# Inverse row transforms at a kernel's end: loads through another queue, five buffers, four ahead, and two groups kept for last

## The chip, the cores and the metric

The kernel runs on one core of a Trainium2 chip. The metric is the device time of one execution in microseconds (us); lower is better. The core has TensorE (PE, with its weight loads listed as PEld), VectorE (DVE), ScalarE (ACT), GpSimd (POOL), and SyncE (SP), which here only issues transfers. All transfers run on the core's 16 DMA engines. An engine works through its own instructions in order; between engines, semaphores are waited for.

## The reference

The input is an image of 48 x 48 tokens with 768 channels in float32. It passes two layers. The first is a transformer block with relative positions and full attention, and an MLP:

```python
xn = layernorm(x, ln1_g, ln1_b)
qkv = xn.reshape(B, H * W, C) @ qkv_w + qkv_b
...
x = shortcut + out
xn2 = layernorm(x, ln2_g, ln2_b)
h = jax.nn.gelu(xn2 @ mlp_w1 + mlp_b1, approximate=False)
return x + (h @ mlp_w2 + mlp_b2)
```

The second, which ends the kernel, goes to the frequencies of rows and columns, applies two small complex matrix layers there in 8 blocks of 96 channels, comes back and adds its input:

```python
xf = jnp.fft.rfft2(x.astype(jnp.float32), axes=(1, 2), norm='ortho')
...
o1r = jax.nn.relu(mm(xr, w1[0]) - mm(xi, w1[1]) + b1[0])
o1i = jax.nn.relu(mm(xi, w1[0]) + mm(xr, w1[1]) + b1[1])
o2r = _softshrink(mm(o1r, w2[0]) - mm(o1i, w2[1]) + b2[0], SPARSITY)
o2i = _softshrink(mm(o1i, w2[0]) + mm(o1r, w2[1]) + b2[1], SPARSITY)
...
y = jnp.fft.irfft2(z.reshape(B, H, Wh, C), s=(H, W), axes=(1, 2), norm='ortho')
return y.astype(x.dtype) + bias
```

## The kernel before

All arithmetic is in float32. A Fourier transform is a matmul with a constant matrix. The tokens stay on the chip throughout in `x1`, 18 tiles of 128 tokens by 768 channels.

**MLP and forward row transforms.** The MLP runs in three passes of 768 tokens. At the end of each, `rows_forward` (L1050) makes the row transform of that pass's tokens: for each half of the channels (384, index k) and each of two groups of 384 tokens, four results `zp` (L1057) from six matmuls. Each is copied to a tile `zt` of 100 x 384 (L1061), of which there are eight, and stored to the DRAM tensor z1 of its half (L1066, z<-zt). In the first two passes ScalarE makes the copies, in the third VectorE and ScalarE in turn.

**Frequencies.** 14 units follow, seven for each half of the channels, each with up to four column frequencies. A unit passes four stages: `columns` (forward column transform, fp at L1178), `first` (first layer, lp at L1197 and L1198), `second` (second layer, mp at L1221) and `back` (inverse column transform, yp at L1240). They are interleaved: round r does `columns` of unit r, `first` of unit r-1, `second` of unit r-2 and `back` of unit r-3, in four steps i of one quarter each. There are 17 rounds. `load` fetches zi from z1 (L926); `back` stores its results y to the DRAM tensor z2 of the half (L1246, z<-y). The last unit of each half has one frequency only, so the last `back` is one yp, in round 16.

**Inverse row transforms.** `rows_back` (L1250) does one group of 384 tokens of one half: a load of 600 KB from z2 to zo (100 partitions x 4 x 384, L1253), then three pieces. A piece is two matmuls into rps (L1261), VectorE's addition of x1 into yt (L1264, four buffers) and a store of 192 KB to the output (L1265). A half has six groups. Because a group needs every frequency of its half, the first half's groups can start once its z2 is complete, during the second half's units, and the second half's groups only after the last yp.

zo has three buffers, and loads and stores all go through SP's queue. `rows_back` is a Python generator that stops after the load and after each piece. `pieces` runs the generators of a half one after another: a group's load is called right before its first piece. The loop takes one such step at each i from round 12 on (L1284), so the first half's groups 0 to 3 are worked off among the second half's units; groups 4 and 5 and the second half's six come after the last yp.

**What sets the order.** TensorE's instructions stand in the order of the Python program (`manual_schedule` for PE). For the other engines and queues a scheduler places the instructions at build time, and gives a tile a buffer of its pool when an earlier tile has been released; the buffers are thus passed on in the order in which the program asks for them. The semaphores of transfers are eight, used in turn, and a transfer also waits for the one that used its semaphore last.

Of the kernel before, what the change touches and what calls it, by code (L numbers as in the profile page):

```python
# [9 lines left out]
F32 = mybir.dt.float32  # L10
# [8 lines left out]
P = 128  # L19
HW = 48  # L20
T = HW * HW
# [8 lines left out]
G = 384  # L30
NB = 8
BS = C // NB
CH = C // 2
KW = HW // 2 + 1
# [10 lines left out]
def block_then_afno(  # L45
# [25 lines left out]
    nc = tc.nc  # L71

    def balanced_copy(i, dst, src):
        if i % 2:
            nc.scalar.copy(dst, src)
        else:
            nc.vector.tensor_copy(dst, src)
# [111 lines left out]
    with ExitStack() as flag_scope:  # L189
# [11 lines left out]
        with ExitStack() as att:  # L201
# [331 lines left out]
            with tc.manual_schedule(engines={mybir.EngineType.PE, mybir.EngineType.SP}):  # L533
# [70 lines left out]
                for n, (pr, c, u) in enumerate(runs):  # L604
# [19 lines left out]
                    if pr < NC - 1:  # L624
                        if (c, u) in ((3, 1), (4, 0), (4, 1)):
                            i = 2 * (2 * (c - 3) + u - 1)
# [55 lines left out]
        with tc.tile_pool(name="ps_flag", bufs=1, space=PSUM) as psum, tc.tile_pool(  # L682
            name="ps_early", bufs=2, space=PSUM
# [29 lines left out]
        with tc.If(safe < 1):  # L713
            with ExitStack() as att:
                xnT = main.rearrange("p (c t) -> p c t", c=NC)
                with tc.tile_pool(name="g_ln1", bufs=3) as ln1, tc.tile_pool(
                    name="g_ps_ln1", bufs=2, space=PSUM
# [197 lines left out]
    turn = ctx.enter_context(tc.tile_pool(name="turn", bufs=6))  # L915
    first_loads = []

    def load_frequencies(half, k0):

        rows = z1[half].rearrange("(r k) c -> r k c", k=KW)  # L920
        tiles = []
        for k in range(k0, min(k0 + 4, KW), 2):
            n = min(2, KW - k)
            zi = turn.tile([P, C], F32, name="zi", tag="turn")
            zi = zi[: 2 * HW].rearrange("p (k c) -> p k c", c=CH)
            nc.sync.dma_start(out=zi[:, :n], in_=rows[:, k : k + n, :])  # L926
            tiles.append(zi)
        return tiles

    with ExitStack() as mlp:  # L930
# [119 lines left out]
        def rows_forward(p):  # L1050

            for k in range(2):
                for g in (2 * p, 2 * p + 1):
                    for a, parts in enumerate(((0,), (1, 2), (3, 4), (5,))):
                        zp = psum.tile([2 * 2 * KW, CH], F32, name="zp", tag=f"o{a}")
                        for b in parts:
                            nc.tensor.matmul(  # L1057
                                zp, rows_dft[:, b, :], x1[:, 3 * g + b // 2, ts(k, CH)],
                                start=(b == parts[0]), stop=(b == parts[-1]),
                            )  # L1060
                        zt = turn.tile([2 * 2 * KW, CH], F32, name="zt", bufs=8)  # L1061
                        if p < 2:
                            nc.scalar.copy(zt, zp)
                        else:
                            balanced_copy(a, zt, zp)
                        nc.sync.dma_start(out=z1[k][ts(4 * g + a, 4 * KW), :], in_=zt)  # L1066
                if (p, k) == (2, 0):
                    first_loads.extend(load_frequencies(0, k0) for k0 in (0, 4))
# [21 lines left out]
        with tc.manual_schedule(engines={mybir.EngineType.PE}):  # L1090
            for p in range(T // TB):
                for n in range(n_f):
                    work = hidden(p, n)
                    for i in range(3):
                        next(work)
                        if n:
                            added(p, n - 1, i)
                    if p < 2 and 4 <= n < 10:
                        normalised(p + 1, n - 4)
                for i in range(3):  # L1100
                    if p < 2:
                        turned(i)
                    added(p, n_f - 1, i)
                if p < 2:
                    sums_of_tokens(xt, xs)
                rows_forward(p)

    with ExitStack() as sp:
        psum = sp.enter_context(tc.tile_pool(name="ps_spec", bufs=2, space=PSUM))
        cst = sp.enter_context(tc.tile_pool(name="spec_const", bufs=1))  # L1110
        zin = sp.enter_context(tc.tile_pool(name="spec_in", bufs=2))
# [137 lines left out]

        def rows_back(half, g):  # L1250

            zo = zin.tile([4 * KW, 4, CH], F32, name="zo", bufs=3)
            nc.sync.dma_start(  # L1253
                out=zo, in_=z2[half][ts(g, 16 * KW), :].rearrange("(a p) c -> p a c", a=4)
            )
            yield
            for i in range(3):
                yt = mid.tile([P, CH], F32, name="yt", bufs=4)
                rp = psum.tile([P, CH], F32, name="rps", tag="f")
                for e in range(2):  # L1260
                    nc.tensor.matmul(  # L1261
                        rp, irows[:, 2 * i + e, :], zo[:, i + e, :], start=(e == 0), stop=(e == 1)
                    )
                nc.vector.tensor_tensor(yt, rp, x1[:, 3 * g + i, ts(half, CH)], ALU.add)  # L1264
                nc.sync.dma_start(out=out[ts(3 * g + i, P), ts(half, CH)], in_=yt)  # L1265
                yield

        units = [Unit(half, k0) for half in range(2) for k0 in range(0, KW, 4)]
        ends = [[rows_back(half, g) for g in range(T // G)] for half in range(2)]

        def pieces(gens):
            for gen in gens:
                yield from gen

        with tc.manual_schedule(engines={mybir.EngineType.PE}):
            first_half = pieces(ends[0])
            for r in range(len(units) + 3):
                if r < len(units):
                    units[r].load()
                for i in range(4):  # L1280
                    for stage, lag in (("back", 3), ("second", 2), ("first", 1), ("columns", 0)):
                        if 0 <= r - lag < len(units):
                            getattr(units[r - lag], stage)(i)
                    if r > len(units) // 2 + 4:  # L1284
                        next(first_half, None)
            for _ in first_half:
                pass
            for _ in pieces(ends[1]):
                pass


# [126 lines left out]
```

## Time and profile before

| | us |
|---|---|
| median of 3 runs | 2955.97 |
| lowest and highest of these | 2951.86, 2956.34 |
| profiled execution, its own time | 2962.34 |
| span from its first to its last instruction | 2960.5 |
| TensorE busy | 2902.6 |
| VectorE busy | 1768.2 |
| ScalarE busy | 881.1 |
| GpSimd busy | 610.2 |
| mean granted clock of TensorE | 0.995 of full speed |

The profile is one execution. Busy times of different engines lie beside one another; they don't add up to the span. The counts of PE are of passes: a matmul in float32 is two, so a piece of the inverse row transforms appears as four. The page divides the span into 40 slices of 74 us, with a digit for each in tenths busy. A finer view gives, for stretches of one's choice, the busy time of each engine, the granted clock and the DMA share. The chain of waits goes back from the last instruction, at each step to what released it. In a list of waits, the name behind the arrow is what ended the wait.

### The profile page before, as it was taken

To read this page: it belongs to the slowest core of one execution; us is meant where nothing else is said; L and a number is where in the kernel's file an instruction comes from. 1 tells how busy PE (TensorE), PEld (TensorE's weight loads), DVE (VectorE), ACT (ScalarE), POOL (GpSimd) and SP (SyncE) were. 2 spreads that over 40 slices of the span, in tenths; PEclk is the share of its full clock that TensorE was granted. 3 is DMA by queue.
4 is the path that set the end of the run, shared out by engine and by line. 5 is a ranking of instruction groups with operands and counts; after the bars stand their busy time and mean duration, and the time that the engine had idled before them with its cause. 6 is when DMAs were issued, how large, how long until landed. Compare 5 with 4: busy or idle time off the path is not lost. (4 is left out here: it accounts for less than half of the span.)

```text
span 2960.5 us, 40962 instructions
## 1 busy us (share of the span) xinstructions
PE 2902.6 (98%) x15771; PEld 1762.2 (60%) x15771; DVE 1768.2 (60%) x2548; ACT 881.1 (30%) x1372; POOL 610.2 (21%) x564
## 2 busy tenths in 40 slices
PE   6999999999999999999999999999999999999998
PEld 4555655555556555555555555555555555557995
DVE  4342327777777777777633666675666566665443
ACT  1011125555556555565500210122011211111210
POOL 2302110000000000000043223342332323322441
PEclk9999999999999999999999999999999999999999
DMA  3423275173461725535252111112111211213225
GB/s 119 150 83 123 88 163 123 26 135 64 75 132 33 139 42 97 113 50 89 59 177 75 42 54 54 64 62 68 54 64 60 75 49 64 64 57 93 83 83 174
DMA packets 202817, 253.03 MB, mean 85 GB/s; under 512 B 21618, under 2 KB 180978, under 8 KB 201078
## 3 DMA queue, kind: packets, MB, share of 16 engines
q1 hardware_dynamic: 202614, 250.32, 33.2%
q8 instruction: 127, 2.08, 0.3%
q14 instruction: 76, 0.62, 0.1%
HBM read 136.40 MB, written 50.14 MB: 63 GB/s over the span
## 5 line engine op out<-in xcount | busy, mean ns | idle before, releaser
L619 DVE TENSOR_TENSOR acc<-acc,main 128x768 f32<-128x768 f32 x576 | 551.9, 958 | 202.0 <-ACT main L562 145.4
L562 ACT ACTIVATE main<-sp 128x768 f32<-128x768 f32 x648 | 522.1, 811 | 155.8 <-PE sp L558 148.6
L558 PE MATMUL sp<-terms,select 64*128 64x384 f32 x1296 | 413.1, 630 | 0.0
L1032 DVE TENSOR_TENSOR main<-o,main 128x384 f32<-128x384 f32 x540 | 299.4, 556 | 41.0 <-PE o L1030 2.1
L970 PE MATMUL h<-shared,w 128*128 128x384 f32 x864 | 296.6, 486 | 0.8 <-issue 0.8
L552 PE MATMUL sp<-shared 64*128 64x384 f32 x1296 | 267.9, 490 | 2.2 <-DVE o L452 2.2
L552 PE MATMUL sp<-qT,kT 64*128 64x384 f32 x1296 | 266.5, 487 | 0.0
L597 POOL TENSOR_TENSOR inverse<-inverse,rden 128x384 f32<-128x384 f32 x36 | 46.3, 1287 | 1031.6 <-DVE rden L594 961.6
L441 PE MATMUL m<-main 128*128 128x384 f32 x756 | 248.4, 490 | 6.2 <-DVE main L172 2.9
L970 PEld LDWEIGHTS h<-shared,w 128*128 128x128 f32 x864 | 164.4, 190 | 116.1 <-issue 2.2
L970 PE MATMUL h<-shared,w1s 128*128 128x384 f32 x648 | 226.6, 486 | 0.0
L567 PE MATMUL op<-main,shared 128*64 128x384 f32 x1296 | 221.3, 488 | 0.0
L567 PE MATMUL op<-main,v 128*64 128x384 f32 x1296 | 219.9, 488 | 0.0
L441 PEld LDWEIGHTS m<-main 128*128 128x128 f32 x756 | 143.4, 191 | 108.7 <-issue 10.1
L976 ACT ACTIVATE hT<-c,vec 128x384 f32<-128x384 f32 x108 | 66.4, 615 | 466.1 <-DVE c L982 466.0
L982 DVE TENSOR_TENSOR c<-h,u 128x384 f32<-128x384 f32 x108 | 60.2, 557 | 212.4 <-PE h L970 212.4
L1030 PE MATMUL o<-w,hT 128*128 128x384 f32 x432 | 175.2, 487 | 3.7 <-DVE mv L118 2.0
L1030 PE MATMUL o<-w2s,hs 128*128 128x384 f32 x432 | 174.9, 487 | 1.4 <-DVE hs L155 1.3
L558 PEld LDWEIGHTS sp<-terms,select 64*128 64x128 f32 x1296 | 125.6, 187 | 84.1 <-issue 0.5
L970 PEld LDWEIGHTS h<-shared,w1s 128*128 128x128 f32 x648 | 123.1, 190 | 85.9
L154 POOL TENSOR_TENSOR w1s<-w 128x384 f32<-128x384 f32 x36 | 36.2, 1006 | 612.5 <-PE o L1030 420.8
L552 PEld LDWEIGHTS sp<-shared 64*128 64x128 f32 x1296 | 117.7, 187 | 60.3 <-issue 23.1
(150 smaller groups left out, 3892.3 us busy)
## 6 DMA issues: line engine op xcount, KB each, us to landing
w<-in_mlp_w_dram SPq DMA_DIRECT2D x72, 768.0 KB
terms<-col_parts SPq DMA_DIRECT2D x432, 72.0 KB
terms<-row_hi SPq DMA_DIRECT2D x216, 72.0 KB
terms<-row_lo SPq DMA_DIRECT2D x216, 72.0 KB
main<-in_qkv_w_dram SPq DMA_DIRECT2D x36, 384.0 KB
z<-zt SPq DMA_DIRECT2D x48, 150.0 KB
zo<-z SPq DMA_DIRECT2D x12, 600.0 KB
x<-in_x_dram SPq DMA_DIRECT2D x18, 384.0 KB
```

Of the source, the lines that this page charges most:

```text
L441: nc.tensor.matmul(bank, a[:, c, :], b[:, c, :], start=(first and c == 0), stop=(c == 2), skip_group_check=not first,)
L552: nc.tensor.matmul(sp[:, j, :G], kT[at, ts(kt, P)], qT[at, ts(c, G)], start=True, stop=False,)
L558: nc.tensor.matmul(sp[:, j, :G], select[at, a % 2], ready[pr, c][at, a // 2, b], start=False, stop=True,)
L562: nc.scalar.activation(p, sp[:, :, :G], AF.Exp, scale=HD**-0.5)
L567: nc.tensor.matmul(op[ts(j, 64)], v[:, kt0 + i, ts(j, 64)], ps[i][:, j, :], start=(kt0 + i == 0), stop=(kt0 + i == NT - 1),)
L597: nc.gpsimd.tensor_tensor(inverse, inverse, rden, ALU.add)
L619: nc.vector.tensor_tensor(acc, made[0] if kt == 1 else acc, p, ALU.add)
L970: nc.tensor.matmul(bank[i], a[:, c, :], b[:, c, :], start=(start and c == 0), stop=(c == 2), skip_group_check=not start,)
L976: nc.scalar.activation(h[:, i, ts(k, G)], src, AF.Gelu, bias=col(V_B1 + 2 * n + i))
L982: nc.vector.tensor_tensor(t, src, other, ALU.add)
L1030: nc.tensor.matmul(bank[k], a, b, start=start, stop=True, skip_group_check=not start)
L1032: nc.vector.tensor_tensor(dst, bank[k], dst, ALU.add)
```

## The change

The loads of the second half's groups are issued by ScalarE in place of SP. Groups whose number over both halves (0 to 11), modulo 5, is 1 or 3 take their zo from a second pool tag, "zt", with two buffers, the others from the three there were. To make these fit, the four zt tiles of a group in `rows_forward` become one tile of 128 x 4 x 384 with two buffers (the same memory as eight); the copies and stores are as before. `in_turn` takes the place of `pieces`: it calls the first loads (two for the first half, four for the second), then after each group's third piece the load of the group so many places on. The loop calls the first half's loads at round 12, step 3, and takes a piece at steps 0 to 2 of rounds 13 to 16. After the loop, the first loads of the second half are called, then what is left of the first half is run, then the second half.

```diff
@@ rows_forward @@
             for k in range(2):
                 for g in (2 * p, 2 * p + 1):
+                    zt4 = turn.tile([P, 4, CH], F32, name="zt", bufs=2)
                     for a, parts in enumerate(((0,), (1, 2), (3, 4), (5,))):
...
-                        zt = turn.tile([2 * 2 * KW, CH], F32, name="zt", bufs=8)
+                        zt = zt4[: 2 * 2 * KW, a]
@@ rows_back @@
-            zo = zin.tile([4 * KW, 4, CH], F32, name="zo", bufs=3)
-            nc.sync.dma_start(
+            if (T // G * half + g) % 5 in (1, 3):
+                zo = turn.tile([P, 4, CH], F32, name="zo2", tag="zt", bufs=2)[: 4 * KW]
+            else:
+                zo = zin.tile([4 * KW, 4, CH], F32, name="zo", bufs=3)
+            (nc.scalar if half else nc.sync).dma_start(
                 out=zo, in_=z2[half][ts(g, 16 * KW), :].rearrange("(a p) c -> p a c", a=4)
             )
@@ the loop at the end @@
-        def pieces(gens):
-            for gen in gens:
-                yield from gen
+        def in_turn(gens, ahead):
+
+            for gen in gens[:ahead]:
+                next(gen)
+            yield
+            for g, gen in enumerate(gens):
+                for _ in range(3):
+                    next(gen)
+                    yield
+                for gen in gens[g + ahead : g + ahead + 1]:
+                    next(gen)
 
         with tc.manual_schedule(engines={mybir.EngineType.PE}):
-            first_half = pieces(ends[0])
+            first_half, second_half = in_turn(ends[0], 2), in_turn(ends[1], 4)
             for r in range(len(units) + 3):
...
-                    if r > len(units) // 2 + 4:
-                        next(first_half, None)
+
+                    if (r, i) == (len(units) - 2, 3) or (r > len(units) - 2 and i < 3):
+                        next(first_half)
+            next(second_half)
             for _ in first_half:
                 pass
-            for _ in pieces(ends[1]):
+            for _ in second_half:
                 pass
```

## The prediction, made before the changed kernel was timed

> Names: a0 to a5 are the six groups of inverse row transforms of the first half of the channels, b0 to b5 those of the second. A group is one 600 KB load (zo<-z), three pieces of two matmuls into rps, three additions on VectorE into yt and three stores. Times are positions in the profiled execution of the kernel before.
>
> **What bounds the kernel now.** First the page: its busy times, and the slices by which to find the one place where TensorE isn't full.
>
> ```profile
> PE 2902.6 (98%) x15771; PEld 1762.2 (60%) x15771; DVE 1768.2 (60%) x2548; ACT 881.1 (30%) x1372; POOL 610.2 (21%) x564
> PE   6999999999999999999999999999999999999998
> ```
>
> TensorE sets the time, and the change removes none of its matmuls: it can only win TensorE's gaps. So next the stretch tables (stretch; length; busy PE, PEld, DVE, ACT, POOL; granted clock; DMA share; GB/s), of the last 60 us and then finer:
>
> ```profile
> 2895.90:2915.90 20.00, 20.00 (x128) 14.36 (x127) 9.35 (x22) 3.05 (x8) 6.14 (x9) 1.00 0.50 158
> 2915.90:2957.20 41.30, 35.53 (x97) 19.15 (x95) 13.50 (x25) 0.00 (x0) 0.00 (x0) 0.92 0.63 207
> ...
> 2800.00:2820.00 20.00, 20.00 (x167) 18.73 (x166) 8.84 (x20) 4.71 (x12) 7.90 (x10) 1.00 0.44 128
> 2820.00:2840.00 20.00, 20.00 (x174) 18.41 (x173) 9.40 (x21) 4.37 (x11) 8.94 (x12) 1.00 0.35 100
> ...
> 2942.00:2944.00 2.00, 2.00 (x5) 1.09 (x4) 0.01 (x1) 0.00 (x0) 0.00 (x0) 0.50 0.62 218
> 2944.00:2946.00 2.00, 2.00 (x4) 1.09 (x4) 0.55 (x1) 0.00 (x0) 0.00 (x0) 0.50 0.37 134
> ```
>
> TensorE is full until 2915.9, where the frequency work ends and only row transforms are left; after that it has gaps, and around 2943 half the clock. The chain of waits and the wait list name the cause:
>
> ```profile
> 2913.49 0.65 PE yp L1240 x2
> 2914.14 1.29 PE rps L1261 x4
> 2915.43 0.65 PE yp L1240 x2
> 2916.08 6.16 PE rps L1261 x20
> 2922.24 6.90 DMA zo<-z
> 2929.28 3.87 PE rps L1261 x12
> 2933.14 7.78 DMA zo<-z
> 2941.06 5.47 PE rps L1261 x8
> 2946.55 0.57 DVE yt L1264
> 2947.14 0.33 SPq L1265
> 2947.56 5.38 DMA zo<-z
> ...
> PE rps L1261 <- DMA zo<-z: 5.8, 5, 2.2
> ```
>
> The reader is to see that a piece takes 1.29 us and a group 3.87, and that a load takes 5.4 to 7.8 us. From the last inverse column matmul (yp) on, eight groups are left: 24 x 1.29 = 31.0 us from 2915.9, so without gaps they would end at 2946.9. They end at 2956.9 (the last starts at 2953.07, plus 3.87). The loss is 10.0 us: 5.8 in the five waits for loads, 3.3 because the 24 passes from 2941.06 take 11.17 us in the timeline where two groups take 7.7 (and 0.16 of draining), and the rest, 1 us, the pipe running empty five times. This 10 us, 0.34%, is all that the change can win.
>
> **What the Trainium skill says.** TensorE: Matmul & The Clock Gate, Part 1, says the clock falls to half after an idle window of about 3.4 us and returns after about as much sustained work. The trace has half clock for some 6 us after waits of 1.35 and 2.2 us shortly after one another, so shorter idleness was enough here. DMA: Bandwidth & Descriptors, Issuing engines are not separate DMA queues, says a second issuing engine saves issue time only, since all transfers run on the same 16 DMA engines; its section Queues, rings and completion order says an engine alternates between the queues that have work, packet by packet. No run here shows that yet: before, all goes through SP's queue (q1).
>
> **The change part by part.**
>
> *Three pieces later.* The order of the built program has nine pieces ahead of the last yp where before had twelve. A piece among the frequency work costs 1.32 us (1.29 to 1.36 in the chain), so the last yp starts 4.0 us earlier: 2915.3 becomes 2911.3. Behind it stand a3 to a5 and b0 to b5, 27 pieces or 34.8 us, from 2912.0: again 2946.8 without gaps. By itself this moves nothing and gives the loads of b 3.9 us more cover. Round 12 without pieces isn't exposed: rounds without pieces are as full (20.00 of 20 in 2820:2840).
>
> *Five buffers.* a0 to a4 are all loaded near 2813 to 2827 instead of three. Two more 600 KB loads stand in front of two zi loads on SP; DMA share there is 0.44 and 0.35 and zi loads run rounds ahead. Nothing. But the order of allocation matters. The three zo buffers go to a0, a2, a4, b1, b3, a5, b4 in the order in which the program reaches them, since the loads of b0 to b3 are called before a5's. So a5 takes a4's buffer: in the built program its load on SP waits for TensorE's count 21596, the one that the addition of a4's third piece waits for. It also stands behind that piece's store on SP, and waits for the semaphore that b0's load counts on. TensorE's order is fixed: a5 directly after a4, b0 after that. a5 is thus loaded with nothing ahead of it.
>
> That wait is the new one. a4 ends at 2912.0 + 6 x 1.29 = 2919.7. The last z<-y store was issued 1.5 us after the last yp and landed within 1.9 (2916.76 in the timeline, the load behind it issued at 2918.70), so b0's load is issued at 2914.7; its predecessor took 6.1 us (2918.70 to 2924.84), so it lands at 2920.8. SP reaches a5's load after the addition and store, 0.2 + 0.6 + 0.4 us after a4: 2920.9. So a5's load is issued near 2921.0, while three loads of b are under way on ScalarE's queue. Not shown by before; bounded by 5.4 us (the last load before, almost alone) and, from above, by being served behind all of those (below). I take 7.8, the longest shown, with other loads and stores in flight. It lands at 2928.8: a gap of 9.1 us. The clock then falls surely; I take 2.5 us for it, between half of 3.4 (the page) and 3.3 (before). Behind the waiting a5 all of b is queued on TensorE, and VectorE and the stores follow TensorE.
>
> *Loads through ScalarE, four ahead.* ScalarE has no compute behind them, and six issues at about 0.3 us, SP's price, lie beside TensorE. b0 to b3 land during the gap. b4 starts when a5 is done and b5 when b0 is; each has four groups, 15.5 us, against 7.8. Two stores (b1's third, b3's first) wait for the semaphore of b4 and b5, at most 1 us late. So the 10.0 us of before go, all five waits.
>
> *Four copies per zt buffer.* The first copy of a group now waits for all four stores of the group two earlier. A store lands 2.3 us after its copy (chain: 2688.92, 2.33). In the last pass the fourth copy of the first group ends at 2685.0, so 2687.4 against a first copy of the third group at 2689.1; the first pass has 1998.3 against 2000.0. 1.7 us spare: nothing, and if a store took over 4 us, the excess would be added up to twice in each of three passes.
>
> Sum: -10.0 + 9.1 + 2.5 = +1.6 us. The profiled execution took 2962.34 us around its span of 2960.5; the three runs shown have a median of 2955.97. I carry the difference over: 2957.5. Without the profile the losses of before may be smaller than 10 us, which speaks for a little more, not less.
>
> **Rivals.**
> 1. Slower, at a5's load: the DMA engines serve it behind b1, b2 and b3, which were issued earlier. For it: they are queued by 2917, and TensorE stands until it lands. Against: the page says queues alternate. Price: 5.4 us alone, less some 2 us fixed (from the small store above), is 3.4 for the data; four of those from 2920.9 end at 2934.5. Gap 14.8 + 3.3 = 18.1, so +8.1: 2964. It is slower beyond 0.2% once the load takes over 11.4 us.
> 2. A short gap: the load takes 5.4 us and the clock is back in 3.4 us: 2926.4 - 2919.7 + 1.7 = 8.4, so -1.6: 2954.4. For it: no stores compete while TensorE stands. Against: three other loads do.
> 3. The change does what it says, and a5's load doesn't count: -10, 2946. The program's wait excludes it: at least 5.4 us of gap stay.
>
> **How the numbers follow.** Two medians of this kernel can be told apart from about 0.2%, 5.9 us: 2950.1 to 2961.9. Forecast 0.62 (2955 to 2961); rival 1 0.24; rival 2 0.13; rival 3 0.01. The low end is rival 2 less the spread of the runs (2951.86 to 2956.34): 2952.5; the high end reaches rival 1's 2964. Slower: most of rival 1 and a tail of the forecast, 0.25; faster: rival 3 and a low draw of rival 2, 0.06; same 0.69.
>
> **What would show it.** Right: one wait of rps on zo of 7 to 10 us, directly before a5, half clock after it, no other wait on zo over 0.5 us, a4's last pass near 2919.7 and the span's end within 3 us of before's. Wrong: no such wait (then -8 or better); a wait of over 11 us; waits of ACT or DVE zt on z<-zt; waits before b4 or b5.

## The result, and the profile after

| | before | changed |
|---|---|---|
| median of 11 runs each, us | 2954.93 | 2963.98 |
| lowest and highest, us | 2946.63, 2957.76 | 2961.59, 2974.04 |
| profiled execution, its own time, us | 2962.34 | 2964.83 |
| its span, us | 2960.5 | 2963.0 |

The ratio over all runs is 1.0036, with an interval of 1.0028 to 1.0044 (the two medians alone give 1.0031): the change costs some 9 us, more than the 0.2% that the prediction took as clear of noise. That is the time of rival 1 of the prediction, 2964, and not its forecast of no change; how much of rival 1's reason holds is taken up below.

The page of the changed kernel looks like the one before. Apart from the first slice, where nothing was changed (7 tenths for 6), only the last slice of TensorE differs (7 tenths, where before had 8):

```profile
span 2963.0 us, 40947 instructions
PE 2897.5 (98%) x15771; PEld 1760.8 (59%) x15771; DVE 1768.7 (60%) x2548; ACT 881.6 (30%) x1372; POOL 608.9 (21%) x564
PE   7999999999999999999999999999999999999997
```

Now the chain of waits of the changed kernel (start in us, length, what), from the last inverse column matmul (yp) to the end:

```profile
2904.99 1.29 PE yp L1241 x4
2906.28 2.60 PE rps L1265 x8
...
2909.48 5.74 DMA out_dram<-yt
...
2915.34 0.57 DVE yt L1268
...
2915.93 0.33 SPq L1269
...
2916.35 11.07 DMA zo<-z
...
2927.55 7.49 PE rps L1265 x12
...
2935.65 6.25 DMA out_dram<-yt
...
2942.02 0.57 DVE yt L1268
...
2942.64 17.05 PE rps L1265 x52
```

Before, this stretch showed load after load, of 5.4 to 7.8 us each. Now a single load carries it: that of a5, issued by SP at 2916.35 right behind the store of a4's third piece, and 11.07 us under way. Behind it three pieces take 7.49 us in place of 3.87. The wait list for the same stretch (engine, line, releaser: us in total, times, longest) and the stretch table (stretch; length; busy PE, PEld, DVE, ACT, POOL; granted clock; DMA share; GB/s) say the same:

```profile
PE rps L1265 <- DMA zo<-z: 13.5, 1, 13.5
...
DVE yt L1268 <- DMA out_dram<-yt: 4.5, 2, 2.5
...
PE rps L1265 <- DVE yt L1268: 1.2, 1, 1.2
```

```profile
2918.00:2920.00 2.00, 0.00 (x0) 0.00 (x0) 0.00 (x0) 0.00 (x0) 0.00 (x0) 0.50 0.66 245
2924.00:2926.00 2.00, 0.00 (x0) 0.00 (x0) 0.00 (x0) 0.00 (x0) 0.00 (x0) 0.50 0.67 244
2930.00:2932.00 2.00, 2.00 (x4) 1.00 (x3) 0.56 (x1) 0.00 (x0) 0.00 (x0) 0.50 0.04 14
```

Before had five waits for loads, 5.8 us; now there is one, of 13.5. While TensorE and everything else stand still, the DMA engines move 245 GB/s: the loads of b1, b2 and b3 beside that of a5. The granted clock is down to 0.50 during the stall; when TensorE goes on it does so at half the clock, and then hardly anything is left to move.

A number serves for all that follows: **the loss**. It is the end of the last row transform, less the end of the last yp, less 1.29 us for each piece that stands behind that yp (24 in the kernel before, 27 in the changed one). For before it is 2957.19 - 2916.08 - 30.96 = 10.1 us (2957.19 is where the last group ends in its chain, 2953.07 + 4.12); for the changed kernel 2959.69 - 2906.28 - 34.83 = 18.6. The difference, 8.4 us, is nearly all of the 9 us of the medians. The rest of the two profiles doesn't count: the changed kernel's last yp ended 9.8 us earlier, but in five profiles whose frequency work is in the same order (before, and four experiments below) that yp ended anywhere from 2908.07 to 2917.04, and the profile of before drew one of the latest.

### The profile page after: what moved, and what is told of

It is laid out like the page before. It is cut to its first block, busy times and chain, and to the rows that moved or that the text cites. A ratio compares the mean times of both kernels' runs of the same rounds, so it can differ in the third digit from the quotient of the medians.

```text
span 2963.0 us, 40947 instructions
## 1 busy us (share of the span) xinstructions
PE 2897.5 (98%) x15771; PEld 1760.8 (59%) x15771; DVE 1768.7 (60%) x2548; ACT 881.6 (30%) x1372; POOL 608.9 (21%) x564
```

## The experiments

In all of them the arithmetic is the kernel's own. The first theory (theory 1 below) is the prediction's own wait with the longer load of rival 1: the order of the loads gives a5 the buffer of a4, so its load starts only when a4 is done, and by then the loads of b1 to b3 are in the DMA engines. Its rivals: the loads through ScalarE's queue disturb the rest whatever the order; the grouped zt costs time; or the stores, not the loads, are what is late.

Medians are in us; "loss" is read from the profile of each, which is one execution. The first four experiments have one set of runs of the kernel before beside them (median 2953.75), the next four another (2955.11), the last four a third (2954.61).

| kernel | median | ratio to before, interval | loss |
|---|---|---|---|
| before | | 1 | 10.1 |
| changed | 2963.98 | 1.0036 (1.0028 to 1.0044) | 18.6 |
| three loads of the first half ahead (e1) | 2951.85 | 0.9988 (0.9982 to 0.9995) | 6.3 |
| second half three ahead (e2) | 2963.31 | 1.0024 (1.0014 to 1.0034) | 13.3 |
| before + ScalarE's queue (e4) | 2951.17 | 0.9988 (0.9981 to 0.9994) | 4.5 |
| b1 to b3 loaded behind a5 (e7) | 2958.69 | 1.0015 (1.0005 to 1.0026) | 12.6 |
| before + one zt tile (e3) | 2953.63 | 1.0000 (0.9991 to 1.0009) | 7.3 |
| e1, all loads on SP (e6) | 2960.09 | 1.0017 (1.0005 to 1.0028) | 15.4 |
| e1 + eight yt (e9) | 2943.32 | 0.9958 (0.9945 to 0.9971) | 1.4 |
| e4 + eight yt (e10) | 2950.15 | 0.9981 (0.9973 to 0.9989) | 2.9 |
| changed + eight yt (e11) | 2961.14 | 1.0020 (1.0014 to 1.0026) | 15.4 |
| e6 + eight yt (e12) | 2952.63 | 0.9991 (0.9984 to 0.9999) | 6.8 |
| e9, one group more inside the loop (e13) | 2947.85 | 0.9978 (0.9967 to 0.9989) | 2.3 |
| before + eight yt (e14) | 2957.06 | 1.0001 (0.9992 to 1.0009) | 8.7 |

Sorted by ratio, the kernels are all but sorted by loss: most of what these edits do, they do behind the last yp.

**e1: three loads of the first half ahead.** Then a5's load is called before those of the second half, so it takes another buffer and comes early. Nothing else moves.

```diff
-            first_half, second_half = in_turn(ends[0], 2), in_turn(ends[1], 4)
+            first_half, second_half = in_turn(ends[0], 3), in_turn(ends[1], 4)
```

> One number of the changed kernel: the first half's loads are called three ahead in place of two, so a5's load is called before those of b0 to b3 and takes a0's buffer instead of a4's. Theory 1 (order of buffers): the wait of rps on zo before a5 (13.5 us) and the half clock after it (3 us) go; nothing of them comes back elsewhere; TensorE runs from the last yp to its end with under 2 us lost, against 18.4 in the changed kernel and 10.0 before. Time about 2946 us, 16 to 18 under the changed kernel and 7 to 10 under before. Rival (transfers): what costs is that four loads of 600 KB through a second queue crowd out the stores and each other; then the wait moves to b0 to b3 or to VectorE's waits for the stores of yt, and the time stays above 2955.

The wait for a5 is gone, and with it 12 us: 2951.85 against 2963.98. But the time lies between the theory's 2946 and the rival's 2955, and 6.3 us are still lost, where the theory left under 2. The wait list and the chain of e1 show where:

```profile
DVE yt L1268 <- DMA out_dram<-yt: 8.3, 6, 3.2
...
PE rps L1265 <- DVE yt L1268: 2.3, 2, 2.1
```

```profile
2909.37 7.19 DMA out_dram<-yt
...
2916.68 0.57 DVE yt L1268
...
2917.29 5.50 PE rps L1265 x8
```

A store takes 7.19 us while loads of b are under way. yt has four buffers, so VectorE waits for a store, TensorE for VectorE (2.1 us), and the next two pieces take 5.50 us, where 2.58 is their full speed. The order of the loads is thus the cause of the 9 us; behind it stands a second loss, of the kind that the rival named.

**e2: three ahead for the second half.** a5 no longer takes a4's buffer but a2's, free long before.

```diff
-            first_half, second_half = in_turn(ends[0], 2), in_turn(ends[1], 4)
+            first_half, second_half = in_turn(ends[0], 2), in_turn(ends[1], 3)
```

> The other number: the second half's loads three ahead in place of four, the first half's two ahead as in the changed kernel. b3 no longer takes a buffer before a5, so a5 gets a2's, free long before; but its load still stands on SP's queue behind the store of a3's third piece, one group (3.9 us) earlier than in the changed kernel, and behind the loads of b0 to b2. Theory 1: a wait before a5 remains, shortened by the 3.9 us and by one load ahead of it in the DMA engines (about 2.6 us): some 7 us; half clock after it stays. Time about 2955 to 2958. Rival (transfers): hardly shorter than 13.5 us, since the same traffic surrounds it; time over 2961.

The chain of waits of e2:

```profile
2911.24 12.06 DMA zo<-z
...
2923.43 6.37 PE rps L1265 x12
```

The load is issued 5.1 us earlier than in the changed kernel, and still takes 12.06 us; TensorE waits 9.4 us, where some 7 were expected, and comes back at half the clock. The wait was longer because the load was slower, not because it was issued later. The time, 2963.31, is the one that the rival gave, and the interval of its ratio overlaps that of the changed kernel. So the buffer is one half of the matter, and how long a load takes beside others is the other half.

**e7: the loads of b1 to b3 behind a5's.** a4 and a5 share a buffer of their own, so a5's load still starts when a4 is done; but b1 to b3 now wait for it to land. One step of the first half stands ahead of the second half's loads.

```diff
-                zo = zin.tile([4 * KW, 4, CH], F32, name="zo", bufs=3)
-            (nc.scalar if half else nc.sync).dma_start(
+                own = not half and g >= 4
+                zo = zin.tile(
+                    [4 * KW, 4, CH], F32, name="zo4" if own else "zo", bufs=1 if own else 2
+                )
+            load = (nc.scalar if half else nc.sync).dma_start(
...
+            if (half, g) == (0, 5):
+                held.append(load)
+            if half and g in (1, 2, 3):
+                tc.add_manual_dep(
+                    load.ins, held[0].ins.name,
...
+            next(first_half)
             next(second_half)
```

> The changed kernel with a5 tied to a4's buffer on purpose (a pair of their own, one buffer; two for the others) and the loads of b1 to b3 made to wait until a5's load has landed. So a5's load still starts when a4 ends, but has only b0's before it in the DMA engines. If the changed kernel's a5 load took 11.1 us because it was served behind b1 to b3: here it takes 5.4 to 6.5 us, the wait before a5 is 6 to 8 us, time about 2957 to 2959. If a load at this place takes 11 us anyway (the second queue, the reading of what was just written): the wait stays at 12 to 14 us and the time at 2963 or more.

The chain of waits of e7, from a4's last pieces to a5's first:

```profile
2912.53 7.76 PE rps L1280 x24
...
2920.30 7.11 DMA zo<-z
...
2927.55 2.92 PE rps L1280 x4
```

With stores, and only the last 0.08 MB on ScalarE's queue, beside it the load takes 7.11 us, a little more than the 5.4 to 6.5 expected. So 4.0 us of the 11.07 were b1 to b3. This is the disputed cost measured by itself; the wait falls to 7.3, and the time is in the range expected. The whole kernel still loses 12.6 us, since the second half's loads now come late and its stores hold VectorE for 11.2 us.

**e4: ScalarE's queue alone.** The kernel before, with one edit.

```diff
-            nc.sync.dma_start(
+            (nc.scalar if half else nc.sync).dma_start(
```

> The kernel before with one part of the change: the second half's loads go through ScalarE's queue; three buffers, pieces one after another, eight zt buffers as before. Theory 1: a second queue alone takes the loads out from behind the stores on SP, which saves the waits behind SP's order (about 1 to 3 us of the 10.0 lost), while three buffers still make each load start only when a group ends: 2950 to 2954. Rival (transfers): loads through ScalarE's queue delay the stores and the time rises to 2957 or more.

Faster by 0.12% (0.06 to 0.19%), as theory 1 expected: the queue is no harm, it is a gain. The waits for loads shrink to 1.0 us; VectorE now waits for stores, twelve times, 13.5 us together, of which TensorE feels 1.7.

**e3: one zt tile alone.** The kernel before, with the first of the change's edits.

```diff
+                    zt4 = turn.tile([P, 4, CH], F32, name="zt", bufs=2)
...
-                        zt = turn.tile([2 * 2 * KW, CH], F32, name="zt", bufs=8)
+                        zt = zt4[: 2 * 2 * KW, a]
```

> The kernel before with one tile of four zt per group in two buffers, and nothing else of the change. The prediction's step: it costs nothing, ratio within 0.999 to 1.001 (2951 to 2957), no wait of ScalarE or VectorE on a zt's buffer longer than 0.5 us that the kernel before has not. Rival: a group's buffer comes free only with its last store, so the evictions wait; 48 groups at 0.1 to 0.3 us each would be 5 to 14 us, ratio 1.002 to 1.005.

No change, to 0.09%. The grouping is cleared.

**e6: the good order, all loads on SP.** Does the queue matter once the order is right?

```diff
-            (nc.scalar if half else nc.sync).dma_start(
+            nc.sync.dma_start(
```

> As e1 (three loads of the first half ahead), but the second half's loads are issued by SyncE like the stores. Theory 1: SP takes its instructions in order, so the loads of b1 to b3, each waiting for a buffer, hold up the first half's last stores, yt's four buffers run full, and TensorE waits 3 to 8 us: 2955 to 2960, 3 us or more above e1. Rival (the order of the loads and the five buffers are all that counts, the queue nothing): 2950 to 2954 as e1.

It does: 2960.09, at the upper end of what was expected and by the ratios 0.29% above e1. SP's timeline in e6 (start, us, queue, line, what, count) has the loads of b1 to b3 in one row, with a store behind them:

```profile
2907.13 0.32 SPq L1257 DMA_DIRECT2D zo<-z  x1
2907.89 0.33 SPq L1269 DMA_DIRECT2D out_dram<-yt  x1
2908.32 3.12 SPq L1257 DMA_DIRECT2D zo<-z  x3
2911.49 4.87 SPq L1269 DMA_DIRECT2D out_dram<-yt  x4
```

A closer look at its parts (the third of these loads, then the addition whose store stands behind it) and SP's wait list say what held the store:

```profile
2911.17 0.28 SPq L1257 DMA_DIRECT2D zo<-z  x1
...
2908.59 0.56 DVE L1268 TENSOR_TENSOR yt<-rps,main 128x384 f32<-128x384 f32 x1 [0.73 <-PE rps L1265]
...
SPq L1257 <- PE rps L1265: 3.2, 4, 1.8
```

The third load, b3's, takes the buffer of a4 and waits for a4's end, 1.8 us. The addition was done at 2909.15, and its store is issued at 2911.49, 2.3 us later. That is the mechanism expected, but it is the smaller part of the cost. The larger part comes behind the issue, as the chain of e6 shows:

```profile
2911.49 13.50 DMA out_dram<-yt
...
2925.12 0.57 DVE yt L1268
```

The store was under way for 13.50 us; on its queue it stood behind three loads, 1.8 MB. In e1, with the loads on the other queue, the comparable store took 7.19 us. The Trainium skill (DMA: Bandwidth & Descriptors, Queues, rings and completion order) says that a DMA engine takes turns between the queues it has work for: this pair agrees, since a store of 192 KB gets past the loads of another queue in about half the time.

**e9: the good order, eight yt.** e1 left a wait for stores behind yt's four buffers; this gives it four more.

```diff
-                yt = mid.tile([P, CH], F32, name="yt", bufs=4)
+                yt = mid.tile([P, CH], F32, name="yt", bufs=8)
```

> The changed kernel with three loads of the first half ahead (as e1) and yt in eight buffers instead of four. Theory 1 (what e1 still loses after the last yp, 6.1 us, is stores that the four second-half loads delay, seen only through yt's four buffers): the 8.3 us of VectorE's waits for stores go to under 1, TensorE's wait of 2.09 us and the half clock after it (about 2.7 us) go with them, under 2 us are lost after the last yp, and the time is 4 us below e1's, 2946 to 2949. Rival (the stores are delayed as much and the last of them sets the end, or the loss is the loads' own landing): the same 2951 to 2953 as e1, with waits for zo or a longer stretch between the last yt and the span's end.

2943.32: 0.42% faster than before (0.29 to 0.55%), and the fastest of all kernels here. TensorE's timeline behind the last yp (start, us, what, and in brackets the idle time ahead of it):

```profile
2904.44 1.46 PE L1241 MATMUL yp<-zz,shared 96*96 96x384 f32 x4
2905.73 28.55 PE L1265 MATMUL rps<-zo,shared 100*128 100x384 f32 x88
2935.37 6.72 PE L1265 MATMUL rps<-zo,shared 100*128 100x384 f32 x20 [1.09 <-DVE yt L1268]
```

88 passes without a gap, one gap of 1.09 us, 20 passes. The waits for stores are 2.9 us in place of 8.3. Of the gain over e1, 8.5 us by the medians of two different sets, the loss explains 4.9; the rest may be the draw of five runs and isn't settled.

**e10, e11 and e14: eight yt elsewhere.** The same edit on e4, on the changed kernel and on the kernel before tells whether yt alone does it.

> The kernel before with the second half's loads issued by ScalarE (as e4) and yt in eight buffers. VectorE's twelve waits for stores, 13.5 us together in e4, should go to under 2. Theory 1: what e4 loses after the last yp (4.4 us) is mostly these waits, so it falls under 2.5 us and the time is 2 us below e4's, 2948 to 2951. Rival: with three buffers of zo, earlier ends of yt only move the wait to zo (1.0 us in e4), which grows to 3 to 5 us; the time stays at 2950 to 2953.

> The changed kernel with yt in eight buffers instead of four and nothing else. Theory 1 (its loss is a5's late load; the stores only cost it one wait of 1.2 us near the end): the wait for a5's load stays at 12 to 14 us with half clock after it, and the time falls by 1 to 2 us, to 2961 to 2964. Rival (the stores held up by yt are the larger part, as between e1 and e9): 8 us less, 2955 to 2957.

> The kernel before with yt in eight buffers and nothing else. Its five waits are for loads of zo, issued one behind the other on SP and each behind a store, not for yt: theory 1 says no change, 2953 to 2956, ratio 0.999 to 1.000. Rival (stores held up by yt hold up the loads behind them on SP): 2 to 4 us faster, 2950 to 2952.

On before it does nothing (1.0001), as theory 1 said: there the loads are late, not yt. On e4 the waits for stores go and the loss falls from 4.5 to 2.9 (under 2.5 was expected), but the time by only 1 us, within the interval; theory and rival aren't told apart by the time, though the waits for zo grew to 1.5 us and not to the rival's 3 to 5. On the changed kernel the loss falls by 3.1 us and the median by 2.8, more than the 1 to 2 us expected: the wait for yt, 1.2 us, is gone, and the half clock costs 1.9 us in this profile (29.22 us in TensorE's timeline for 84 passes, where 21 x 1.29 and 0.24 for the pipe's end make 27.33), in place of 3.4. The wait for a5 stays whole, as the chain of e11 shows, this time with b0's landing and not the store ahead of it on SP as what let it go:

```profile
2912.65 6.47 DMA zo<-z
...
2919.13 0.02 SPq L1257
...
2919.18 11.50 DMA zo<-z
...
2930.81 29.23 PE rps L1265 x84
```

So the wait for a5's load, which took 11.50 us here, stays the main loss of the changed kernel with eight yt too.

**e12: e9 with all loads on SP.** The edit is that of e6.

> As e9 (three loads of the first half ahead, eight yt), with the second half's loads issued by SyncE instead of ScalarE. Theory 1: the loads of b1 to b3 wait in SP's order for their buffers and hold the stores behind them; four more buffers of yt give 4 x 1.29 = 5.2 us of cover for a wait that was 10.5 us in e6, so some 5 us of it stay: 2950 to 2954, 7 us or more above e9. Rival (with eight yt the queue no longer matters): 2943 to 2946, as e9.

2952.63, 9 us above e9, in the range expected, and for the two reasons found in e6: the store behind the loads is issued 2.3 us late and then takes 12.13 us. With eight yt TensorE waits 4.2 us for that, in place of 9.5.

**e13: one group more inside the loop.** Two groups, not three, are left as cover.

```diff
-                    if (r, i) == (len(units) - 2, 3) or (r > len(units) - 2 and i < 3):
+                    if (r, i) == (len(units) - 3, 3) or (r > len(units) - 3 and i < 3):
```

> As e9, but the first half's pieces begin a round earlier, so that 12 of them, not nine, stand ahead of the last yp, as in the kernel before. Behind it two groups of the first half stay, 6 x 1.29 = 7.7 us, where b0's load in e9 landed 2915.3 - 2905.9 = 9.4 us after the last yp. Theory 1 (the third group is needed as cover): one wait of about 1.7 us for b0's load, 2944 to 2947. Rival (no difference; the load lands sooner with fewer stores beside it): 2942 to 2944.

The wait for b0 that was expected at 1.7 us is 1.63 in TensorE's timeline:

```profile
2906.76 7.91 PE L1265 MATMUL rps<-zo,shared 100*128 100x384 f32 x24
2916.30 19.64 PE L1265 MATMUL rps<-zo,shared 100*128 100x384 f32 x60 [1.63 <-DMA zo<-z]
```

The loss is 1.0 us above e9's. The median, 2947.85, is 4.5 us above e9's and beyond both ranges given, but the intervals of the two ratios overlap slightly: the wait is shown, the size of its cost is not.

## Why the prediction was wrong

**The bound, the place and the cause of the new wait were right.** TensorE sets the time and only its gaps behind the last yp could change. a5 is the one group loaded with nothing ahead of it: the order in which the program asks for buffers gives it a4's. e1, which changes that order by one number, takes the wait away and 12 us with it. All three things named as what the load stands behind appear: a4's end, SP's store of a4 (the chain of the changed kernel), and b0's landing (the chain of e11).

The prediction's own sign of being wrong came with it: one wait of over 11 us (13.5), and no other wait on zo.

**The step that failed is the size of one term: "I take 7.8, the longest shown, with other loads and stores in flight."** The load took 11.07 us, and 11.50 and 12.06 in e11 and e2. With b1 to b3 held back it took 7.11 (e7): 7.8 is near the price of a load with stores and the end of one other load beside it, and not of one that joins two and a half others. The rows of before, with load after load on one queue, had no such place: during its longest load, those 7.78 us, 1.85 MB moved. The bytes give the price. The changed kernel's queues (q10 is ScalarE's, q1 SP's: packets, MB, share of 16 engines) moved, from the issue of a5's load to its landing (2916.35 to 2927.42), and in the five microseconds in which most of a5's data went through (2920 to 2925):

```profile
q10 hardware_dynamic: 1026, 1.53, 38.1%
q1 hardware_dynamic: 726, 1.04, 25.7%
...
q1 hardware_dynamic: 408, 0.61, 33.6%
q10 hardware_dynamic: 406, 0.61, 33.0%
```

In all 2.57 MB moved: what was left of b1 to b3, a5's 0.61 MB, and 0.4 MB of stores ahead of it on SP's queue. At the 245 GB/s of the stall that is 10.5 us, by my estimate, against 11.07. In e11 it was 2.58 MB in 11.50 us, in e2 3.05 MB in 12.06, and in e7 1.36 MB in 7.11.

The argument against rival 1, that queues alternate, was right, as the last two lines show: the two queues moved the same 0.61 MB side by side, so a5 was not served behind b1 to b3. But at half of 245 GB/s its data alone takes 5 us, some 3.6 us had gone by before 2920, with stores ahead of it on SP's queue, and its last packets and the landing took the rest. The prediction named the sharing and didn't price it: its 7.8 is the time of fewer bytes.

**The sum beside what was measured.**

| term | predicted, us | measured, us |
|---|---|---|
| losses of before that go | -10.0 | -10.1 |
| from a4's end to the issue of a5's load | 1.3 | 2.3 |
| the load | 7.8 | 11.1 |
| half clock after it | 2.5 | 3.4 |
| the wait for yt near the end | 0 | 1.2 |
| together | +1.6 | +7.9 |

a4's end is 2906.28 + 6 x 1.29 = 2914.02. The load's issue came 1.0 us late because the addition ahead of it waited for a store; the half clock is 13.92 us in the timeline for the 32 passes behind the gap, less 10.56 at full speed (8 x 1.29, and 0.24 for the pipe's end: before has 4.11 in the timeline for groups of 3.87). The measured column falls 0.5 us short of 8.4, for the pipe's draining and the rounding of a piece. 3.3 of the 6.3 us by which the sum was off are the load, the largest part. By itself it would have made 2960.8 of the 2957.5, still within the 0.2%: the prediction put the point of decision at a load of 11.4 us, with 3.3 for the clock. It took the later issue, the clock and the wait for yt besides to go past it. Rival 1 had a gap of 14.8 and 3.3 for the clock, where 13.5 and 3.4 were measured. Its 2964 was met to the microsecond with some luck: its reason, that a5 is served behind b1 to b3, isn't what happened, and the wait for yt made up for the shorter gap.

**The other steps.** "Last yp 4.0 us earlier": can't be read from one profile each, since the profiles scatter by 9 us and more ahead of it. The eight with nine pieces ahead (changed, e1, e2, e6, e7, e9, e11, e12) have a mean of 2906.3, the six with twelve 2912.0: 5.7 us, with a scatter that doesn't exclude 4.0. It is no gain by itself, as said. Grouped zt at nothing: shown by e3. The wait list of the changed kernel does name the stores of zt, with 21.6 us of ScalarE's time, which was to be a sign of being wrong; but 20.1 of them are one wait that was as long before (20.1 us, put down there to zp), so nothing was added. ScalarE's issues at nothing, and the loads of b landing during the gap: right. "At most 1 us late" for two stores: near the end VectorE waited 2.5 us for a store and TensorE 1.2 us for that; e1 and e9 show that the stores slowed by the loads, seen through yt's four buffers, are a cost of this scheme, which the prediction didn't have as a term. Half clock after the gap: seen. The section cited there, TensorE: Matmul & The Clock Gate, Part 1, asks for an idle window of about 3.4 us. In e1 two pieces took more than twice their full-speed time after an idle time of 2.09 us. As before, less idleness was enough here. Nor does the length of one wait decide: 2.21 us were followed by half clock in before, and by full clock in e14 (TensorE's timeline, before and then e14):

```profile
2941.06 11.17 PE L1261 MATMUL rps<-zo,shared 100*128 100x384 f32 x24 [2.21 <-DMA zo<-z]
...
2942.71 4.11 PE L1261 MATMUL rps<-zo,shared 100*128 100x384 f32 x12 [2.21 <-DMA zo<-z]
```

What decides between them isn't settled here.

**Carrying over the 6.4 us was right in the main.** Most of the difference between before's profiled execution and the median lay ahead of the last yp, which came late in that execution. But the losses of before are 10.1, 8.7 and 7.3 us in three profiles with the same order at the end (before, e14, e3), so the 10 us to be won was a high draw too, as the prediction suspected; with the mean of the three, 8.7, the measured loss of 18.6, itself one profile, makes 9.9 us, and the medians say 9.

## What to carry to other kernels

Where buffers are handed on in the order in which a program asks for them, write down for each load whose buffer it gets; a prefetch called ahead of an older group's load takes that group's early buffer, and the older group then waits for its direct predecessor. Price a transfer by all the bytes that are in the DMA engines when it starts, over the rate that the trace shows, not by the longest time in a trace that never had so many at once. When loads are brought forward, count the buffers of the stores too: here the reordered loads gained 0.12% over the kernel before, and 0.42% once the output tiles could wait out the slower stores, while the same buffers did nothing for the kernel before.

## What the runs showed of the hardware

A store of 192 KB took 13.50 us when it was issued on the same queue right behind three loads of 600 KB, and 7.19 us when these were on the other queue. Two queues with work shared the DMA engines evenly: 0.61 MB each in 5 us of the changed kernel's stall. The Trainium skill says that a second issuing engine saves only the time of issuing (DMA: Bandwidth & Descriptors, Issuing engines are not separate DMA queues). For these runs that is too little: the second queue was worth 0.12% with the order of before (e4), and 0.33% between e12 and e9. SP's order held a store back by 2.3 us in e12; the larger part was the 12.13 us that it then took.

The DMA engines' share stayed at 0.66 to 0.67 in the stall of the changed kernel, with nothing else to move and 245 GB/s. So with these loads of 100 partitions alone to move, a third of the engines' time went unused; in e9, with stores of 128 partitions among them, the share reached 0.96 and 360 GB/s. That the partitions are the reason wasn't tested. The stretch of e9:

```profile
2928.00:2930.00 2.00, 2.00 (x8) 1.21 (x7) 0.98 (x2) 0.00 (x0) 0.00 (x0) 1.00 0.96 360
```
